# Four graph layers: layer 2's third step in T tiles, layer 3's results back to tokens by VectorE and DRAM

## The chip, the cores and the metric

The kernel runs on one core of one Trainium2 chip. The metric is the device time of one execution in microseconds, from a few runs; the median of three runs of the kernel before is 3717.38 us (3716.55 to 3718.34). A core has five engines that run their own instruction queues: TensorE (matmuls, PE in the profile), VectorE (DVE), ScalarE (ACT), GpSimd (POOL) and SyncE (SP), which here issues the DMAs.

## The reference

`x` is 64 graphs of 256 nodes with 256 features, `adj` their 0/1 adjacency. Four layers follow each other, each on h = relu(layernorm(x)), and each adds its result to x. Layer 0 is attention with 8 heads, layer 1 a graph attention with one head. What the change touches is layer 2 (a gated graph network of three steps) and layer 3 (graph attention with 4 heads of 64 features):

```python
def _gru_cell(inp, h, w_ih, w_hh, b_ih, b_hh):
    gi = inp @ w_ih.T + b_ih
    gh = h @ w_hh.T + b_hh
    i_r, i_z, i_n = jnp.split(gi, 3, axis=-1)
    h_r, h_z, h_n = jnp.split(gh, 3, axis=-1)
    r = sigmoid(i_r + h_r); z = sigmoid(i_z + h_z)
    n = tanh(i_n + r * h_n)
    return (1.0 - z) * n + z * h
# layer 2
for i in range(3):
    m = jnp.einsum('bnd,de->bne', h, weight[i])
    aggr = jnp.einsum('bst,bsd->btd', A, m)
    h = _gru_cell(aggr, h, w_ih, w_hh, b_ih, b_hh)
# layer 3
f = (einsum('bni,oi->bno', h, W) + b).reshape(B, N, H, c)
logits = leaky_relu(s_src[:, :, None, :] + s_dst[:, None, :, :], 0.2)
probs = softmax(where(adj[..., None] == 1, logits, -9e15), axis=2)
out = einsum('bijh,bjhc->bihc', probs, f).reshape(B, N, H * c)
```

## The kernel before

The 64 graphs go through in 32 pairs. A pair has 512 nodes, held as four groups of 128 (`T = 4`); half g of a pair is one graph. A "token" tile `[128, 4*256]` has nodes on the partitions and features along the row; a "T" tile `[128, 2*512]` has features on the partitions and the 512 nodes along the row. The matmuls are in float32 except the adjacency products of layer 2, which split h into three bfloat16 parts.

Nothing in the code gives the final order directly. Each layer function records tasks with `add` (engine, expected duration, buffers read and written), and `Plan.order` (L110) builds the order: at each point it takes, of the ready tasks, the one that by the planner's own model can begin first, with ties decided by a key. The key is the pair's number times `PERIOD` plus an offset per layer and kind of engine (`ON_PE`, `ON_SP`, `OTHERS`). `SLOW`, `MARGIN`, `BACK` and `SPARE` shape DMA latency, waits of SyncE, the choice between VectorE and GpSimd, and spare buffers; `RANKS` says where the preparation of the weights falls. A task with two forms (`evict`, `either`) can go to either of two engines, and the plan decides which. So several pairs are in work at the same time, and each engine has one fixed queue. SyncE issues all DMAs: inputs, outputs, rows broadcast to all partitions (`to_all`), and the turns.

A **turn** is a transposition of a whole `[128, 1024]` tile without TensorE. VectorE transposes blocks of 32x32 (`nc.vector.transpose`, L617 or L636), and `through_dram` (L603) writes the tile to a DRAM buffer (one DMA, L606) and reads it back so that the blocks change places (four DMAs, L609). Layer 0 uses eight a pair, layer 3 four, and layer 2 uses `turn_chunks` (L632) after its first two steps, so 14 a pair; the last pair uses TensorE in layers 2 and 3 (L1046, L627). A tile from `turn_chunks` has its columns in another order, marked `mixed`.

Layer 2, steps one and two, run in T form: `gate` (L964) makes a bank of gate sums for 128 features by 512 nodes, with the weights as the stationary operand, and the bias enters as a value per partition in ScalarE's activation (L981, L993, L1009, L1021). VectorE forms the rest (L998, L1005, L1026, L1031), and either GpSimd or VectorE the subtraction (L1014). The third step runs in token form (from L1052): the node tile is the stationary operand and the weights stream (L1066), 512 columns wide for r and z, 256 wide for the new gate. Biases then lie along the row and are added by VectorE from broadcast tiles `brz_bc` and `bhn_bc` (L1082, L1095, L1116). Half g needs only its own node groups, and its result goes straight into x (L1121, L1126, L1128, L1133).

Layer 3 (L1138) computes f for each group of nodes (L1159), makes the logits (Prelu, L1189), masks them and takes the row extreme (L659), exponentiates (L666), turns the result, and multiplies with f (L1211), which leaves features on the partitions. That product is evicted (L321), transposed to tokens by four TensorE transposes per half (`back`, L1227), multiplied by the reciprocal sums of the softmax (L1234), and added to x (L1239). The last pair runs a finer variant (`hT.fine`, `last`).

Of the kernel before, what the change touches and what calls it, by code (L numbers as in the profile page):

```python
# [16 lines left out]
P = 128  # L17
# [21 lines left out]
class Plan:  # L39
# [11 lines left out]

    SPARE, GRAIN = 4, 0.01
    SLOW, MARGIN = 1.3, 0.2
    BACK = {"DVE": 0.8, "POOL": 1.3}


    PERIOD, REST = 260.1, 0
    ON_PE = (128, 788, 5100, -4300)  # L60
    ON_SP = (3449, 2192, 2058, -4527)
    OTHERS = (100, -16, -1143, 1788)

    def __init__(self, slots, spare):
        self.slots, self.spare = slots, spare
# [121 lines left out]
def tile_adj_preln_d4(  # L187
# [43 lines left out]
        "f3": (2, [P, T, E3], FP, 0),  # L231
        "mask": (4, [P, T * N], BF, 1),
        "ps": (8, [P, 512], FP, 2),
        "w2": (4, [P, N2], FP, 2),
        "st": (4, [P, T, 6], FP, 1),
        "mv": (4, [P, T, 2], FP, 1),
        "rs": (4, [P, 2, T], FP, 1),
# [4 lines left out]
        "rows": (3, [T * H3, P], FP, 0),  # L242
        "dst": (4, [P, T, H3], FP, 0),
        "turn": (8, [P, T * N], FP, 0),
        "row1": (4, [N2], FP, 0),
        "row3": (4, [H3 * N2], FP, 0),
    }
# [13 lines left out]
    def held(name, shape):  # L261
        return const.tile(shape, FP, name=name)
# [6 lines left out]
    giT = held("giT", [P, NL, 2, 3 * D])  # L269
    whhT = held("whhT", [P, 2, 3 * D])  # L270
    brz, bhn, bih_sb, bhh_sb = held("brz", [P, 4]), held("bhn", [P, 2]), held("bih_sb", [P, 6]), held("bhh_sb", [P, 6])

    brz_bc = held("brz_bc", [P, N2])
    bhn_bc = held("bhn_bc", [P, 2, D])
    a1_sb = held("a1_sb", [P, 2, 2])
    blk = held("blk", [P, 2, 2, H3])
    nc.vector.memset(blk, 0.0)
# [4 lines left out]
    dram = ctx.enter_context(tc.tile_pool(name="dram", bufs=1, space=bass.MemoryType.DRAM))  # L282
    for tag, (n, shape, dtype, _) in SLOTS.items():
        if tag not in tiles:
            tiles[tag] = [(dram if tag in ("row1", "row3", "turn") else work).tile(shape, dtype, name=f"{tag}_{i}") for i in range(n)]
    plan = Plan({tag: v[0] for tag, v in SLOTS.items()}, {tag: v[3] for tag, v in SLOTS.items()})

    def buf(tag):
# [2 lines left out]
    def w4():  # L291
        return buf("w4")
# [7 lines left out]
    def dve(n):  # L300
        return 0.065 + n / 960.0
# [82 lines left out]
    def weights2():  # L384
# [45 lines left out]
        def halved():  # L430
# [5 lines left out]
        bhh_bc = w4()  # L436
        load_rows(brz_bc, b_ih[0:N2], (BN, 2))
        row = b_hh[0:N2]
        load(
            lambda: bhh_bc()[:, 0:N2],  # L440
            bass.AP(tensor=row.tensor, offset=row.offset, ap=[[0, P], [1, N2]]), bhh_bc,
        )
        add((V, dve(N2), lambda: nc.vector.tensor_add(brz_bc, brz_bc, bhh_bc()[:, 0:N2]), True), reads=[bhh_bc], writes=[(BN, 2)])
        load_rows(bhn_bc[:, 0], b_ih[N2 : 3 * D], (BN, 3))
        load_rows(bhn_bc[:, 1], b_hh[N2 : 3 * D], (BN, 4))

    def weights3():

# [183 lines left out]
    def turn_chunks(src, dst):  # L632

        e = w4()
        add(
            (V, dve(T * N) + 0.04, lambda: nc.vector.transpose(  # L636
                e().rearrange("p (b i x) -> p b x i", b=4, i=32), src().rearrange("p (x b j) -> p b x j", b=4, j=32))),
            reads=[src], writes=[e],
        )
        through_dram(e, dst)  # L640
        dst.mixed = True
# [268 lines left out]
    def layer2(xt, p):  # L910
# [47 lines left out]
                )  # L958
            return aT

        for l in range(NL - 1):
            r, hn, u = w4(), w4(), w4()

            def gate(us, terms, c0, o, claims=()):  # L964
# [88 lines left out]
        two = lambda ap, g: tok(ap())[:, 2 * g : 2 * g + 2, :]  # L1053

        def state(h, g):
            if h.mixed:
                return h().rearrange("p (m k t) -> p t k m", k=2, t=T)[:, 2 * g : 2 * g + 2]
            return two(h, g).rearrange("p t (k m) -> p t k m", k=2)

        bias = lambda i: bhn_bc[:, i : i + 1, :].to_broadcast([P, 2, D])  # L1060

        def tokens_mm(out, terms, t, c0, n):
            m = 0
            for w, src in terms:
                for k in range(2):
                    mm(out, chunk(src, k, t), w[:, k, c0 : c0 + n], start=m == 0, stop=m == 2 * len(terms) - 1)  # L1066
                    m += 1

        def new_gate(w, src, g, claims=()):
            ps = bank()  # L1070

            def product():
                for c in range(2):
                    tokens_mm(ps()[:, c * D : (c + 1) * D], ((w, src),), 2 * g + c, N2, D)

            add((PE, 1.74, product), reads=[src, HH, GI[l]], writes=[ps], claims=claims)
            return ps

        for g in range(2):
            ps = new_gate(whhT, hT, g, [hn])  # L1080
            add(
                (V, dve(N2), lambda g=g, ps=ps: nc.vector.tensor_tensor(two(hn, g), tok(ps()), bias(1), ALU.add)),  # L1082
                reads=[ps, BN], writes=[(hn, g)],
            )
        aT = messages(h)
        both = ((whhT, hT), (giT[:, l], aT))
        for g in range(2):
            for c in range(2):
                ps = bank()
                add(  # L1090
                    (PE, 3.44, lambda t=2 * g + c, ps=ps: tokens_mm(ps(), both, t, 0, N2)),
                    reads=[hT, aT, HH, GI[l]], writes=[ps], claims=[rz[g]],
                )
                add(
                    (V, dve(N2), lambda g=g, c=c, ps=ps: nc.vector.tensor_tensor(at_o(rz[g], c), ps(), brz_bc, ALU.add)),  # L1095
                    reads=[ps], writes=[(rz[g], c)],
                )
                add(
                    (A, act(N2), lambda g=g, c=c: nc.scalar.activation(at_o(rz[g], c), at_o(rz[g], c), AF.Tanh, scale=0.5)),
                    writes=[(rz[g], c)],  # L1100
                )
            gate_of = lambda g, i: tok(rz[g](), N2)[:, :, i * D : (i + 1) * D]

            add(
                (V, dve(N2), lambda g=g, gate_of=gate_of: nc.vector.scalar_tensor_tensor(
                    two(hn, g), gate_of(g, 0), 1.0, two(hn, g), ALU.add, ALU.mult), True),
                reads=[rz[g]], writes=[(hn, g)],
            )
            ps = new_gate(giT[:, l], aT, g)
            add(  # L1110
                (V, dve(N2), lambda g=g, ps=ps: nc.vector.scalar_tensor_tensor(
                    two(hn, g), two(hn, g), 0.5, tok(ps()), ALU.mult, ALU.add)),
                reads=[ps], writes=[(hn, g)],
            )
            add(
                (V, dve(N2), lambda g=g: nc.vector.tensor_tensor(two(hn, g), two(hn, g), bias(0), ALU.add), True),  # L1116
                writes=[(hn, g)],
            )
            add((A, act(N2), lambda g=g: nc.scalar.activation(two(hn, g), two(hn, g), AF.Tanh)), writes=[(hn, g)])
            add(  # L1120
                either(0.4 if h.mixed else 0.0, lambda eng, g=g: eng.tensor_sub(  # L1121
                    two(df, g).rearrange("p t (k m) -> p t k m", k=2), state(h, g),
                    two(hn, g).rearrange("p t (k m) -> p t k m", k=2))),
                reads=[h, (hn, g)], writes=[(df, g)],
            )
            add(either(0.0, lambda eng, g=g: eng.tensor_add(two(xt, g), two(xt, g), two(hn, g))), reads=[(hn, g)], writes=[(xt, g)])  # L1126
            add(
                (V, dve(N2), lambda g=g, gate_of=gate_of: nc.vector.scalar_tensor_tensor(  # L1128
                    two(df, g), gate_of(g, 1), 1.0, two(df, g), ALU.add, ALU.mult), True),
                reads=[rz[g]], writes=[(df, g)],  # L1130
            )
            add(
                (V, dve(N2), lambda g=g: nc.vector.scalar_tensor_tensor(  # L1133
                    two(xt, g), two(df, g), 0.5, two(xt, g), ALU.mult, ALU.add), True),
                reads=[(df, g)], writes=[(xt, g)],
            )

    def layer3(xt, p):  # L1138
        at, hT = norm_relu_T(xt, p)
# [36 lines left out]
        for g in range(2):  # L1176
# [121 lines left out]
```

## Time and profile before

| | |
|---|---|
| median of 3 runs | 3717.38 us |
| the profiled execution | 3717.08 us |
| its span, first to last instruction | 3715.3 us |
| mean granted TensorE clock | 0.993 |
| L971, gates of steps one and two (TensorE, 3072 records) | 722.1 + 715.1 us busy |
| L1066, all gates of the third step (2048 records) | 242.7 + 240.6 + 121.0 + 120.9 us busy |
| L617, blockwise transposes (VectorE, 380) | 466.3 us busy, mean 1233 ns |
| L636, the transposes of `turn_chunks` (VectorE, 62) | 126.1 us busy, mean 2034 ns |
| turns: DMA to DRAM / back | 442 of 512 KB / 1768 of 128 KB |
| mean share of the 16 DMA engines | 57.8% |

A group's row in the profile has its busy time, the mean duration of one record in ns, and the idle time of that engine just before its instructions, with the releaser that ended most of it. A float32 matmul in the code makes two records. Busy time counts a record from its start to a modelled end, and the next record may begin before that end; the time that a stretch of matmuls takes is read from the starts in the timeline.

### The profile page before, as it was taken

The page shows a single profiled execution, that of the slowest core. Times are in us where ns is not written, and L with a number is a line of the kernel's source. Part 1 is how long each engine was busy: PE and PEld are TensorE (multiplying, and loading weights), DVE is VectorE, ACT ScalarE, POOL GpSimd, SP SyncE. Part 2 cuts the span into 40 slices and gives each one's busy share as a digit, 9 for nine tenths or more (in the row PEclk, how much of TensorE's full clock was granted, in tenths as well). Part 3 has the DMA queues.
Part 4 walks back from the last instruction along what each step waited for, and adds up shares of the span by engine and source line. Part 5 has one row for each costly group of instructions (what it writes and reads, how often), then busy time and mean ns, then how long its engine had stood idle before and what let it go on. Part 6 is the DMA issues. An engine that isn't in the chain of part 4 may idle for free.

```text
span 3715.3 us, 56987 instructions
## 1 busy us (share of the span) xinstructions
PE 3657.9 (98%) x17377; PEld 2186.9 (59%) x17377; DVE 2881.1 (78%) x7648; ACT 2693.9 (73%) x7227; POOL 532.9 (14%) x494
## 2 busy tenths in 40 slices
PE   8999999999999999999999999999999999999997
PEld 5665565555656556565565656556565565655554
DVE  6877777887778877778877779877788777888765
ACT  6986666777677777777877768876777767777545
POOL 2001111111121101112011111111211111121000
PEclk8999999999999999999999999999999999999998
DMA  7783455756456664557646566565566645666322
GB/s 215 198 221 106 132 152 172 199 167 180 137 163 193 190 182 125 165 168 193 187 136 184 154 180 185 163 185 137 163 195 184 176 132 161 189 193 187 100 88 86
DMA packets 443970, 615.21 MB, mean 166 GB/s; under 512 B 44944, under 2 KB 374544, under 8 KB 443664
## 3 DMA queue, kind: packets, MB, share of 16 engines
q1 hardware_dynamic: 443664, 611.57, 57.8%
q8 instruction: 139, 2.28, 0.3%
q14 instruction: 167, 1.37, 0.1%
HBM read 362.56 MB, written 248.84 MB: 165 GB/s over the span
## 4 chain that ended last, share of the span: by engine, by line
PE 72%; ACT 13%; DVE 7%; DMA 5%; issue 1%; SPq 1%; POOL 0%; DVEq 0%; POOLq 0%; ACTq 0%
PE ps L971 24%; PE ps L1066 14%; ACT w L666 6%; PE ps L690 6%; PE ps L582 5%; PE ps L949 4%; PE ps L1159 3%; PE ps L553 3%; PE ps L883 3%; PE ps L710 2%; ACT w L741 2%; DMA w<-turn 2%; PE ps L760 2%; PE ps L1211 2%; PE ps L816 2%; DMA turn<-w 1%
## 5 line engine op out<-in xcount | busy, mean ns | idle before, releaser
L666 ACT ACTIVATE w<-w,mx 128x256 f32<-128x256 f32 x1536 | 758.7, 498 | 15.9 <-DVE mx L659 14.3
L971 PE MATMUL ps<-w,whhT 128*128 128x512 f32 x1536 | 722.1, 596 | 0.7 <-DVE w L1031 0.5
L971 PE MATMUL ps<-w,giT 128*128 128x512 f32 x1536 | 715.1, 594 | 0.0
L321 ACT COPY w<-ps 128x512 f32<-128x512 f32 (+1 forms) x564 | 318.9, 582 | 313.4 <-PE ps L690 99.8
L617 DVE STREAM_TRANSPOSE w<-w 128x1024 f32<-128x1024 f32 x380 | 466.3, 1233 | 66.3 <-ACT w L666 44.2
L659 DVE CUSTOM_DVE_ANT_0 w<-ps,mask 128x256 f32<-128x256 f32 x1024 | 369.5, 417 | 167.1 <-PE ps L710 166.5
L971 PEld LDWEIGHTS ps<-w,giT 128*128 128x128 f32 x1536 | 288.5, 190 | 337.8 <-issue 326.2
L971 PEld LDWEIGHTS ps<-w,whhT 128*128 128x128 f32 x1536 | 277.5, 190 | 279.2 <-issue 256.2
L741 ACT ACTIVATE w<-w,rz 128x256 f32<-128x256 f32 x896 | 381.5, 498 | 2.4 <-DVE rz L734 2.4
L1066 PE MATMUL ps<-whhT,w 128*128 128x512 f32 (+1 forms) x1024 | 363.6, 491 | 0.0
L1066 PE MATMUL ps<-giT,w 128*128 128x512 f32 (+1 forms) x1024 | 356.1, 486 | 0.0
L528 ACT ACTIVATE w<-x,rs 128x256 f32<-128x256 f32 x472 | 247.5, 591 | 96.4 <-DVE rs L520 92.6
L1014 POOL TENSOR_TENSOR w<-w,w 128x512 f32<-128x512 f32 x91 | 122.8, 1350 | 1187.9 <-ACT w L1009 1088.8
L666 ACT ACTIVATION_READ_ACCUMULATOR w<-w,mx 128x1 f32 x1536 | 292.3, 190 | 0.0
L1066 PEld LDWEIGHTS ps<-giT,w 128*128 128x128 f32 x1024 | 193.5, 190 | 149.0 <-issue 134.7
L659 DVE CUSTOM_DVE_ANT_0 w<-w,mask 128x256 f32<-128x256 f32 x512 | 200.5, 417 | 102.1 <-ACT w L1189 102.0
L949 PEld LDWEIGHTS <-w 128*128 128x128 bf16 x2304 | 243.5, 128 | 52.0 <-issue 32.8
L949 PE MATMUL ps<-mask,w 128*128 128x256 bf16 x2304 | 272.5, 274 | 0.0
L1066 PEld LDWEIGHTS ps<-whhT,w 128*128 128x128 f32 x1024 | 189.8, 191 | 116.0 <-issue 99.5
L514 POOL TENSOR_SCALAR rs<-mv 128x4 f32<-128x4 f32 x129 | 55.7, 432 | 1180.0 <-DVE mv L503 1131.9
L501 DVE BATCH_NORM_STATS2 st<-x 128x6 f32<-128x256 f32 x512 | 190.9, 415 | 41.4 <-DMA x<-in_x_dram 38.3
L1189 ACT ACTIVATE w<-w,f 128x256 f32<-128x256 f32 x512 | 222.8, 498 | 0.0
(130 smaller groups left out, 5783.5 us busy)
## 6 DMA issues: line engine op xcount, KB each, us to landing
turn<-w SPq DMA_DIRECT2D x442, 512.0 KB, 3.2
w<-turn SPq DMA_DIRECT2D x1768, 128.0 KB, 4.3
w<-in_adj_dram SPq DMA_DIRECT2D x128, 512.0 KB, 6.3
w<-row SPq DMA_DIRECT2D x64, 512.0 KB, 4.8
x<-in_x_dram SPq DMA_DIRECT2D x64, 256.0 KB, 5.6
out_dram<-x SPq DMA_DIRECT2D x64, 256.0 KB, 2.2
w<-row SPq DMA_DIRECT2D x32, 256.0 KB, 4.7
w<-in_L_gnn_weight_dram SPq DMA_DIRECT2D x3, 256.0 KB, 6.0
```

The source lines that it names most:

```text
L321: (A, act(n), lambda: nc.scalar.copy(dst(), src())),
L501: nc.vector.bn_stats(st()[:, t, :], tok(xt())[:, t, :])
L528: nc.scalar.activation(tok(xn())[:, t, :], tok(xt())[:, t, :], func, bias=rs()[:, 1, t : t + 1], scale=rs()[:, 0, t : t + 1])
L617: add((V, dve(T * N), lambda: nc.vector.transpose(blocks(), blocks())), writes=[e])
L659: nc.vector.tensor_tensor_reduce(row, src, mask, scale, 3.0e38, ALU.add, ALU.min, mn)
L666: nc.scalar.activation(row(e, r), row(e, r), AF.Exp, bias=mn()[:, r : r + 1], scale=-1.0, accum_out=zs()[:, z0(r) : z0(r) + 1])
L690: mm(ps(), w[:, k, o * P : (o + 1) * P], wide(hT, k), start=k == 0, stop=k == 1)
L741: op(row, row, rz()[:, r : r + 1])
L949: mm(ps()[:, g * N : (g + 1) * N], chunk_of(part(), h.mixed, t, o), tok(am(), N)[:, t, :], start=i == 0 and c == 0, stop=i == 2 and c == 1,)
L971: mm(ps(), w[:, k, c0 : c0 + P], wide(src, k), start=n == 0, stop=n == 2 * len(terms) - 1)
L1066: mm(out, chunk(src, k, t), w[:, k, c0 : c0 + n], start=m == 0, stop=m == 2 * len(terms) - 1)
L1189: nc.scalar.activation(dst, src, AF.Prelu, bias=f()[:, t, D + h : D + h + 1], alpha=ALPHA)
```

## The change

Layer 2's third step uses the T form of the first two: the loop runs over all `NL` steps. Its new h returns to tokens as after the other steps (`turn_chunks` for 31 pairs, TensorE transposes for the last), and is then added to x half by half by GpSimd or VectorE. The token form with its broadcast biases and their loads is removed.

In layer 3, for all pairs but the last, the product of a half is no longer transposed by TensorE. VectorE transposes its 32x32 blocks, one DMA writes the tile to a DRAM buffer `turn2`, four DMAs read it back so that nodes are on the partitions, and eight instructions per half (four heads for each of two groups of nodes) multiply by the reciprocal sum and add to x in one go.

The planner's constants are all different, and two more `w2` buffers replace the bias tiles.

```diff
-    SPARE, GRAIN = 4, 0.01
-    SLOW, MARGIN = 1.3, 0.2
-    BACK = {"DVE": 0.8, "POOL": 1.3}
-    PERIOD, REST = 260.1, 0
-    ON_PE = (128, 788, 5100, -4300)
-    ON_SP = (3449, 2192, 2058, -4527)
-    OTHERS = (100, -16, -1143, 1788)
+    SPARE, GRAIN = 5, 0.001
+    SLOW, MARGIN = 1.4, 0
+    BACK = {"DVE": 0.3, "POOL": 0.8}
+    PERIOD, REST = 954.6, 0
+    ON_PE = (-336, 2037, 8685, -4071)
+    ON_SP = (6411, 2547, 4387, -3182)
+    OTHERS = (2416, 34, -17, 3238)
...
-        "w2": (4, [P, N2], FP, 2),
+        "w2": (6, [P, N2], FP, 2),
+        "turn2": (4, [P, N2], FP, 0),
...
-    brz_bc = held("brz_bc", [P, N2])
-    bhn_bc = held("bhn_bc", [P, 2, D])
...
-        load_rows(brz_bc, b_ih[0:N2], (BN, 2))
...
-        load_rows(bhn_bc[:, 0], b_ih[N2 : 3 * D], (BN, 3))
-        load_rows(bhn_bc[:, 1], b_hh[N2 : 3 * D], (BN, 4))
...
-        for l in range(NL - 1):
+        for l in range(NL):
...
             if by_dma(l, p):
                 turn_chunks(u, h)
-                continue
-            for g in range(2):
+            for g in range(2) if not h.mixed else ():
...
-        l, rz, hn, df = NL - 1, [w4() for g in range(2)], w4(), w4()
...
+            if l == NL - 1:
+                for g in range(2):
+
+                    def to_x(eng, g=g, h=h):
+                        ap = h().rearrange("p (m k t) -> p t k m", k=2, t=T) if h.mixed else h().rearrange("p (t k m) -> p t k m", k=2, t=T)
+                        x4 = xt().rearrange("p (t k m) -> p t k m", k=2, t=T)[:, 2 * g : 2 * g + 2]
+                        eng.tensor_add(x4, x4, ap[:, 2 * g : 2 * g + 2])
+
+                    add(either(0.4 if h.mixed else 0.0, to_x), reads=[h if h.mixed else (h, g)], writes=[(xt, g)])
...
             add(evict(N2, oT, pso), reads=[pso], writes=[oT])
+            if not last:
+
+                e2, o, d = buf("w2"), buf("w2"), buf("turn2")
+                add(
+                    (V, dve(N2), lambda oT=oT, e2=e2: nc.vector.transpose(
+                        e2().rearrange("p (b x i) -> p b x i", b=4, i=32), oT().rearrange("p (x b j) -> p b x j", b=4, j=32))),
+                    reads=[oT], writes=[e2],
+                )
+                add((SP, 0.6, lambda d=d, e2=e2: nc.sync.dma_start(d(), e2())), reads=[e2], writes=[d], latency=3.2)
+                for b in range(4):
+                    add(
+                        (SP, 0.55, lambda b=b, d=d, o=o: nc.sync.dma_start(
+                            o()[32 * b : 32 * b + 32, :].rearrange("p (a w) -> p a w", a=4),
+                            d()[:, b * P : (b + 1) * P].rearrange("(a j) w -> j a w", a=4))),
+                        reads=[d], writes=[(o, b)], latency=3.0, claims=[rz],
+                    )
+                for c in range(2):
+
+                    def to_x(c=c, g=g, o=o, rz=rz):
+                        for h in range(H3):
+                            ap = o().rearrange("p (j a x i) -> p j x a i", j=2, a=2, i=32)[:, h % 2, 2 * (h // 2) + c]
+                            xh = tok(xt())[:, 2 * g + c, h * C3 : (h + 1) * C3].rearrange("p (a i) -> p a i", a=2)
+                            nc.vector.scalar_tensor_tensor(
+                                xh, ap, rz()[:, H3 * c + h : H3 * c + h + 1], xh, ALU.mult, ALU.add
+                            )
+
+                    add((V, H3 * 0.14, to_x, True), reads=[o, rz], writes=[(xt, g)])
+                continue
             psq, o = bank(), buf("w2")
...
-    RANKS = (1.7, 2.3, 1.2)
+    RANKS = (2.3, 1, 0.3)
```

More of the change, by code (lines that the diff above doesn't have):

```diff
@@ L284, in tile_adj_preln_d4 @@
         if tag not in tiles:
-            tiles[tag] = [(dram if tag in ("row1", "row3", "turn") else work).tile(shape, dtype, name=f"{tag}_{i}") for i in range(n)]
+            tiles[tag] = [(dram if tag in ("row1", "row3", "turn", "turn2") else work).tile(shape, dtype, name=f"{tag}_{i}") for i in range(n)]
     plan = Plan({tag: v[0] for tag, v in SLOTS.items()}, {tag: v[3] for tag, v in SLOTS.items()})
@@ L435, in weights2 @@
         add((V, 0.2, halved, True), writes=[BN])
-        bhh_bc = w4()
-        load_rows(brz_bc, b_ih[0:N2], (BN, 2))
[L438 to L443, printed above, removed]
-        load_rows(bhn_bc[:, 0], b_ih[N2 : 3 * D], (BN, 3))
-        load_rows(bhn_bc[:, 1], b_hh[N2 : 3 * D], (BN, 4))
     def weights3():
@@ L635, in turn_chunks @@
         add(
-            (V, dve(T * N) + 0.04, lambda: nc.vector.transpose(
+            (V, 1.8, lambda: nc.vector.transpose(
                 e().rearrange("p (b i x) -> p b x i", b=4, i=32), src().rearrange("p (x b j) -> p b x j", b=4, j=32))),
@@ L1049, in layer2 @@
                 add(evict(N2, lambda g=g, h=h: h()[:, g * N2 : (g + 1) * N2], ps), reads=[ps], writes=[(h, g)])
-        l, rz, hn, df = NL - 1, [w4() for g in range(2)], w4(), w4()
[L1053 to L1136, printed above, removed]
```

## The prediction

> **What bounds the kernel now.** I read the engine totals first, then the table of windows (busy time of each engine in stretches of the span), then the groups by line with shapes kept apart, and the timeline at two places.
>
> ```profile
> PE 3657.9 (98%) x17377; PEld 2186.9 (59%) x17377; DVE 2881.1 (78%) x7648; ACT 2693.9 (73%) x7227; POOL 532.9 (14%) x494
> ```
>
> ```profile
> 20.00:40.00 20.00, 17.30 (x113) 12.25 (x111) 12.80 (x68) 11.45 (x35) 1.26 (x2) 0.83 0.89 265
> 40.00:60.00 20.00, 13.26 (x52) 8.35 (x53) 14.54 (x50) 16.83 (x47) 10.02 (x10) 0.66 0.92 260
> ...
> 1600.00:2000.00 400.00, 398.33 (x1893) 239.70 (x1890) 311.19 (x817) 286.75 (x751) 64.80 (x59) 1.00 0.59 167
> ...
> 3640.00:3680.00 40.00, 34.49 (x150) 21.43 (x150) 31.61 (x77) 24.12 (x67) 3.15 (x5) 0.96 0.42 120
> 3680.00:3700.00 20.00, 14.07 (x44) 7.65 (x44) 8.21 (x34) 13.11 (x39) 0.00 (x0) 0.50 0.23 77
> ```
>
> After the times come PE, PEld, DVE, ACT, POOL, the granted clock, the DMA share and GB/s. In the middle TensorE stands still for 1.7 us in 400; of its 57 idle us (3715.3 - 3657.9) 17 lie in the first 60 us and some 21 in the last 75. So in the middle, time goes only where TensorE work goes; VectorE (78%) and ScalarE (73%) have room. But a busy PE row counts modelled ends, so I price TensorE work from start to start of rows that follow without a gap:
>
> ```profile
> L1066 PE MATMUL ps<-whhT,w 128*128 128x512 f32 x512 | 242.7, 596 | 0.0
> L1066 PE MATMUL ps<-giT,w 128*128 128x256 f32 x512 | 121.0, 379 | 0.0
> L1227 PE MATMUL ps<-ident,w 128*128 128x128 f32 x256 | 39.4, 276 | 2.2 <-ACT w L321 1.4 <-DVE w L322 0.8
> ```
>
> ```profile
> 3598.21 1.88 PE L1066 MATMUL ps<-giT,w 128*128 128x512 f32 x4
> 3599.93 0.60 PE L1227 MATMUL ps<-ident,w 128*128 128x128 f32 x4
> 3600.36 1.89 PE L1066 MATMUL ps<-giT,w 128*128 128x256 f32 x8
> 3602.09 1.88 PE L1066 MATMUL ps<-whhT,w 128*128 128x512 f32 x4
> ```
>
> Four matmuls of 512 columns take 1.72 us (0.43 each), eight of 256 take 1.73 (0.216 each), four transposes of 128 take 0.43, though their row says 0.60.
>
> **Layer 3's way back.** In 31 of 32 pairs the two groups of four L1227 transposes go (the last pair keeps its two). 62 x 0.43 = **26.7 us** of TensorE's own queue. By busy time it would be 62 x 39.4/64 = 38.2; I take 26.7, since the next matmul starts inside the row.
>
> [...]
>
> What comes instead, per half of a pair: one VectorE transpose of 128x512, one DMA to DRAM, four back, eight fused multiply-adds of 128x64. No row has the half-size transpose: half of the blockwise transpose L636 (2.034 us) is 1.02, half of the plain one L617 (1.23) is 0.6; L636 has the same pattern, so 62 x 1.02 = 63 us. For the fused instruction, the nearest small row is L520 (128x4, 0.176 us); 60 more elements at the rate of L998 (0.745 for 512) bring some 0.08, so 0.25 apart, less where the next one overlaps: 0.13 to 0.25, taken 0.2, so 496 x 0.2 = 99 us. [...] Either way VectorE pays more here than for what it loses: L1234 (43.2 us) and its part of L1239 (23.8). This costs nothing as long as VectorE stays below TensorE, so I add it up.
>
> **VectorE's sum.** Out with the old third step: L1082, L1095, L1105, L1111, L1116, L1121, L1126, L1128, L1133, together 424 us. In: half of what two steps now take in L998, L1005, L1026, L1031 (382, so 191), 31 turns of 2.03 (63), and the additions of h to x (31 x 1.07, as L1121 strided: 33; three more for L1014). Layer 3: -65, +162. The order of the two programs also shows the planner's re-assignment: 86 more normalizations on VectorE (L534, 0.37: +32), 244 more divisions (L741, 0.305: +74), some evictions (+5). Net +74, so 2955 of some 3690: 80%. ScalarE loses about as much by the same count (244 divisions and 86 normalizations out, 192 Tanh passes of the old step out, 254 biased ones in): -98, 70%. Neither bounds.
>
> **Layer 2's third step.** Before, a pair takes 32 records of 512 columns and 32 of 256: 32 x 0.43 + 32 x 0.216 = 20.7 us. After, 48 of 512: 20.6. Nothing, though there are a quarter fewer matmuls: TensorE pays by column. The weight loads lie under the matmuls in both. The results of 31 pairs return to tokens by the existing DRAM turn; the last pair uses eight more TensorE transposes (0.9 us, in the ending below).
>
> **DMA and SyncE.** Added: 31 whole turns of 0.52 MB each way and 62 half ones, 65 MB on 611.6. At the present rate the share of the DMA engines goes from 57.8 to 64%; the half turns read back in rows of 512 bytes instead of 1 KB, so up to 67%. SyncE's queue gets 465 more issues at 0.34 (L606) and 0.43 us (L609): 191 us, 6 us of a pair's 116. They stand in one queue, in order, with layer 0's and layer 3's turns, adjacency loads and outputs. A blocked head is nothing new there:
>
> ```profile
> SPq L790 <- ACT rows L321: 741.1, 62, 27.6
> SPq L606 <- DVE w L617: 452.4, 180, 41.2
> ```
>
> Yet TensorE waited 1.0 us in all for a turn. The new wait on VectorE is the fused group's, for the DMA back (issue, 3.2 us landing, four issues, 4.3 landing: some 10 us); what stands behind it is every later VectorE instruction, evictions for TensorE among them. Summed with the durations of these rows, VectorE's new order has 11 to 15 us of instructions between most transposes and their fused group, but some 4 to 6 in a tenth of them. So mostly covered; a late one costs up to 5 us on VectorE, at 20% spare. I take 0.
>
> **Smaller terms.** The order has 113 fewer changes from one matmul group to another, 62 of them the removed transposes. A change costs 0 to 0.1 us (a 512-column group after L1211 takes 1.82 instead of 1.72), so -3 (0 to -5). At the start 0.77 MB of broadcast biases go from a stretch where DMA is 0.9 busy: 3 us of transfer at 260 GB/s, mostly not waited for: -1 (0 to -3).
>
> At the end something is lost. Before, the token form finishes half g=0 of the last pair before its last gate matmul, and its layer 3 starts 2.8 us after that (3667.65 to L553 at 3670.45), the other half at 3679.47. In T form all gates must be done before either half returns: Tanh 0.68, two fused steps 1.4, transposes 0.9, eviction 0.6, addition 0.7, statistics 1.2, rstd 1.1, scaling 1.1 and hops. Half 0 is late by some 6 us, half 1 about as before. Pair 30's layer 3 softmax now stands here too (it fills the gap). ScalarE's softmax of half 0 then bounds the tail: **+5** (0 to +10).
>
> **Sum**, on the profiled execution's 3717.1 (span 3715.3 and 1.8 around it): -26.7 - 3 - 1 + 5 = 3691.4; the median of the runs is 0.3 higher, which changes nothing. **3691 us**. What I can't price is the order itself: all planner constants change. Its room for gain is the idle time between 60 and 3640 us, 19 us by the windows; its room for loss is open.
>
> **Rivals.**
> A, as summed: 3691, own range 3678 to 3703. Chance 0.60.
> B, the new order also takes idle time out of filling, middle and ending: all 19 us and no loss at the end gives 3667. For it: those waits hang on ScalarE and VectorE (L528, the mask of L806), whose loads are reshuffled. Against: 1.5 us per 400 is near the floor. 0.20.
> C, the transposes go, but half is given back in short waits because the chain of a pair is two DRAM trips (20 us) longer and buffers are held longer: 3691 + 13 = 3704. Against: pairs overlap. 0.12.
> D, slower: SyncE's queue becomes the limit. A turn that lands late (7.8 us at most against 4.2 in the median) or waits behind the new DMAs stalls TensorE 3.6 us. It decides from 26 us in all, or one stall in every fourth pair; one in every second is 16 x 3.6 = 58, so 3749. Against: SyncE spends most of its time waiting for producers, and fourteen trips a pair (442/32) have left 1.0 us of wait. 0.08.
> That the transposes don't go is excluded: the order holds 8 of 256.
>
> **Chances and range.** A measurement of this kernel tells 0.2% (7.4 us) from no change. Faster (below 3709.9): A and B whole, most of C: 0.87. Same: 0.06, C's and D's edges. Slower: 0.07. The range takes in B's end and C's: 3668 to 3711.
>
> **What would show it.** TensorE's busy time down by some 38 (busy rows) to about 3620, 99% or more in the middle windows, with the same 0.43 for a 512-column record; 8 transposes on the old back line; VectorE near 80% and fused rows of 0.13 to 0.25 us; DMA at 64 to 67%; longer idle time in the last 60 us. It is wrong if TensorE's waits for DMA or for VectorE in the middle windows exceed a few us per 400, or if the 512-column records of the third step don't run at 0.43.

## The result, and the profile after

| | before | after |
|---|---|---|
| median of 4 runs | 3717.86 us (3716.55 to 3719.21) | 3682.09 us (3680.70 to 3684.02) |
| the profiled execution / its span | 3717.08 / 3715.3 us | 3682.95 / 3681.2 us |
| mean granted TensorE clock | 0.993 | 0.993 |

The ratio is 0.9904 (95% interval 0.9887 to 0.9921): **35.8 us faster**, where 26.4 were forecast (3691 against 3717.4). So the direction and the range hold, and a quarter of the gain has no place in the sum. The engine totals of the kernel after, busy time first:

```profile
PE 3620.5 (98%) x16625; PEld 2056.2 (56%) x16625; DVE 2912.0 (79%) x8192; ACT 2573.7 (70%) x6950; POOL 529.0 (14%) x512
q1 hardware_dynamic: 510048, 675.82, 64.0%
```

TensorE's busy time is 37.4 us lower (38 forecast), VectorE's share 79%, ScalarE's 70%, and the queue of DMAs has 64.0% of 16 engines' span. All four were forecast to within a point. To find what was not forecast, the table of windows is the view to read. Its stretches are chosen here to separate the start, the filling, the middle and the ending. First the kernel before:

```profile
0.00:60.00 60.00, 42.61 (x192) 26.94 (x193) 33.78 (x145) 35.27 (x92) 19.64 (x26) 0.83 0.82 241
60.00:800.00 740.00, 733.54 (x3618) 441.70 (x3616) 576.92 (x1580) 556.45 (x1522) 92.89 (x88) 1.00 0.58 165
800.00:3400.00 2600.00, 2588.36 (x12344) 1546.58 (x12344) 2056.46 (x5450) 1933.82 (x5197) 397.39 (x356) 1.00 0.60 171
...
3534.00:3715.30 181.30, 160.08 (x631) 92.23 (x629) 108.00 (x249) 88.95 (x226) 10.32 (x12) 0.92 0.28 85
```

and the kernel after, in the same view:

```profile
0.00:60.00 60.00, 42.16 (x208) 27.43 (x209) 39.66 (x157) 40.38 (x112) 19.61 (x26) 0.89 0.82 237
60.00:800.00 740.00, 732.64 (x3497) 419.59 (x3496) 596.63 (x1698) 526.01 (x1446) 93.19 (x89) 1.00 0.63 180
800.00:3400.00 2600.00, 2600.00 (x11991) 1475.26 (x11990) 2110.78 (x5928) 1864.57 (x5049) 389.57 (x371) 1.00 0.67 192
...
3500.00:3681.20 181.20, 145.71 (x544) 79.08 (x542) 101.71 (x265) 87.80 (x220) 10.03 (x11) 0.91 0.36 106
```

TensorE's idle time is the stretch less the first busy figure. Over the whole span it hardly moves, 57.4 us before and 60.7 after, but it has changed its place. At the start it is 17.4 and 17.8, in the filling 6.5 and 7.4. In the middle it falls from 11.6 us to nothing at all: TensorE never waits in 2600 us. In the last 181 us it grows from 21.2 to 35.5. A total of idle time would have hidden both movements.

The second measure is the period, the time from one pair to the next in the middle. After, it can be read from the chain of waits, whose rows have the start, the duration and the number of joined steps. The same stretch of gates comes back 111.52 us later, which is 2157.84 - 2046.32:

```profile
2046.32 12.02 PE ps L959 x28
...
2157.84 12.02 PE ps L959 x28
```

Before, even and odd pairs follow at unequal distances, so I take a mean over 20 pairs (from the seventh to the twenty-seventh, by the starts of layer 1's product): 113.30 us. The same reading of the kernel after gives 111.52 again. A pair is 1.78 us cheaper, and the eight removed transposes should make only 0.86 of it (8 x 0.108). **The rest of this 1.78 is what the experiments look for.**

The rows of the new work, from the groups on VectorE with shapes kept apart:

```profile
L1154 DVE SCALAR_TENSOR_TENSOR x<-w,rz,x 128x64 f32<-128x64 f32 x496 | 105.4, 279 | 0.7 <-DMA w<-turn 0.7
L1136 DVE STREAM_TRANSPOSE w<-w 128x512 f32<-128x512 f32 x62 | 42.4, 685 | 26.2 <-ACT w L319 26.2
```

The fused instruction's records have a mean of 279 ns, but they overlap: 105.4 us over 496 are 0.21 us each. VectorE waited for the way back through DRAM 0.7 us in all, in a row that covers 31 pairs.

The ending shows what the larger idle time is. TensorE's timeline after the last gates (start, duration, and in brackets the idle time before, with its releaser):

```profile
3620.88 1.88 PE L959 MATMUL ps<-w,giT 128*128 128x512 f32 x4
3622.59 0.27 PE L1033 MATMUL ps<-ident,w 128*128 128x128 f32 x1
3625.05 0.98 PE L1033 MATMUL ps<-ident,w 128*128 128x128 f32 x7 [2.18 <-DVE w L1019]
3637.57 2.25 PE L541 MATMUL ps<-ident,w 128*128 128x128 f32 x8 [11.54 <-ACT w L516]
```

For 11.54 us TensorE waits for the last pair's normalization (L516), ahead of its layer 3. The timelines of ScalarE, GpSimd and VectorE, in this order, show why it is so late:

```profile
3626.59 3.70 ACT L1099 ACTIVATE w<-w,f 128x256 f32<-128x256 f32 x9
...
3634.13 2.89 ACT L1099 ACTIVATE w<-w,f 128x256 f32<-128x256 f32 x7
3636.92 1.08 ACT L516 ACTIVATE w<-x,rs 128x256 f32<-128x256 f32 x2
```

```profile
3628.53 0.75 POOL L503 TENSOR_TENSOR rs<-rs,mhalf 128x2 f32<-128x2 f32 x1
3632.10 0.23 POOL L502 TENSOR_SCALAR rs<-mv 128x2 f32<-128x2 f32 x1 [2.83 <-DVE mv L491]
```

```profile
3633.46 0.12 DVE L508 SCALAR_TENSOR_TENSOR rs<-mv,rs 128x2 f32<-128x2 f32 x1
```

GpSimd has the first half's reciprocal deviation ready at 3629.3 (3628.53 + 0.75). Meanwhile ScalarE works through pair 30's logits (L1099) and exponentials, and VectorE through its masks and a turn. These come first in their fixed queues. So VectorE takes the next step of pair 31 (L508) only at 3633.46, and ScalarE begins its scaling (L516) only at 3636.92. From the start of the last gate matmul to the start of the last matmul it was 41.6 us before and is 53.5 now. Before, the last gates, the first transposes of the last pair behind them, and the end were these:

```profile
3664.11 3.61 PE L1066 MATMUL ps<-giT,w 128*128 128x512 f32 x12
...
3670.45 0.33 PE L553 MATMUL ps<-ident,w 128*128 128x128 f32 x1 [0.85 <-ACT w L528]
...
3708.58 0.66 PE L1227 MATMUL ps<-ident,w 128*128 128x128 f32 x4 [0.69 <-ACT w L321]
```

### The profile page after: what moved, and what is told of

Read it like the earlier page. It is cut to its first block, busy times and chain, and to the rows that moved or that the text cites. A ratio compares the mean times of both kernels' runs of the same rounds, so it can differ in the third digit from the quotient of the medians.

```text
span 3681.2 us, 56370 instructions
## 1 busy us (share of the span) xinstructions
PE 3620.5 (98%) x16625; PEld 2056.2 (56%) x16625; DVE 2912.0 (79%) x8192; ACT 2573.7 (70%) x6950; POOL 529.0 (14%) x512
## 3 DMA queue, kind: packets, MB, share of 16 engines
q1 hardware_dynamic: 510048, 675.82, 64.0%
## 4 chain that ended last, share of the span: by engine, by line
PE 95%; ACT 2%; DVE 2%; DMA 1%; issue 0%; SPq 0%; DVEq 0%; ACTq 0%
PE ps L959 53%; PE ps L937 7%; PE ps L678 6%; PE ps L570 6%; PE ps L698 3%; PE ps L1069 3%; PE ps L1121 3%; PE ps L541 3%; PE ps L748 3%; PE ps L871 3%; PE ps L804 3%; ACT w L654 1%; PE ps L414 0%; DVE w L647 0%; ACT w L729 0%; PE ps L830 0%
## 5 line engine op out<-in xcount | busy, mean ns | idle before, releaser
L959 PE MATMUL ps<-w,whhT 128*128 128x512 f32 x2304 | 1083.7, 599 | 3.3 <-DVE w L1019 2.5
L959 PE MATMUL ps<-w,giT 128*128 128x512 f32 x2304 | 1068.4, 593 | 0.0
L959 PEld LDWEIGHTS ps<-w,giT 128*128 128x128 f32 x2304 | 433.0, 190 | 521.5 <-issue 487.9
L959 PEld LDWEIGHTS ps<-w,whhT 128*128 128x128 f32 x2304 | 418.8, 190 | 460.9 <-issue 438.1
L319 ACT COPY w<-ps 128x512 f32<-128x512 f32 x546 | 308.6, 580 | 181.5 <-PE ps L937 56.7
L997 ACT ACTIVATE w<-w,bih_sb 128x512 f32<-128x512 f32 x192 | 135.3, 717 | 287.0 <-DVE w L993 286.9
L729 ACT ACTIVATE w<-w,rz 128x256 f32<-128x256 f32 x652 | 284.8, 499 | 1.5 <-DVE rz L722 1.5
L981 ACT ACTIVATE w<-ps,brz 128x512 f32<-128x512 f32 x192 | 130.4, 679 | 202.9 <-PE ps L959 202.9
L986 DVE SCALAR_TENSOR_TENSOR w<-w,w 128x512 f32<-128x512 f32 x192 | 131.5, 685 | 146.1 <-ACT w L981 145.8
L516 ACT ACTIVATE w<-x,rs 128x256 f32<-128x256 f32 x386 | 206.3, 593 | 42.8 <-DVE rs L508 40.5
L1099 ACT ACTIVATE w<-w,f 128x256 f32<-128x256 f32 x512 | 227.9, 499 | 2.9 <-DMA w<-row 2.9
L553 ACT ACTIVATE w<-ps 128x512 f32<-128x512 f32 x184 | 102.7, 595 | 167.2 <-PE ps L541 167.0
L1009 ACT ACTIVATE w<-ps,brz 128x512 f32<-128x512 f32 x192 | 129.2, 673 | 128.3 <-PE ps L959 128.2
```

What stands on the lines that cost most here:

```text
L319: (A, act(n), lambda: nc.scalar.copy(dst(), src())),
L516: nc.scalar.activation(tok(xn())[:, t, :], tok(xt())[:, t, :], func, bias=rs()[:, 1, t : t + 1], scale=rs()[:, 0, t : t + 1])
L729: op(row, row, rz()[:, r : r + 1])
L959: mm(ps(), w[:, k, c0 : c0 + P], wide(src, k), start=n == 0, stop=n == 2 * len(terms) - 1)
L1099: nc.scalar.activation(dst, src, AF.Prelu, bias=f()[:, t, D + h : D + h + 1], alpha=ALPHA)
```

## Experiments

**The structure without its planner constants, and the constants without the structure.** First the whole new structure with the constants of before, and the old structure with the new ones.

```diff
-    SPARE, GRAIN = 5, 0.001
-    SLOW, MARGIN = 1.4, 0
+    SPARE, GRAIN = 4, 0.01
+    SLOW, MARGIN = 1.3, 0.2
...
-    ON_PE = (-336, 2037, 8685, -4071)
+    ON_PE = (128, 788, 5100, -4300)
...
```

> The whole change in structure, planned with the constants of the kernel before. Theory 1 (the gain is TensorE's removed transposes, whatever the order): 31 pairs x 0.9 us less, so about 3690 us, middle period of a pair near 112.4 us. Theory 2 (half of the steady gain is the new order, which took TensorE's gaps out): above 3695, gaps of 1 to 3 us per 400 us stay, as before.

> The structure of the kernel before, planned with the new constants. Theory 1: within some 8 us of 3718, since no TensorE work goes. Theory 2: the order alone takes gaps away, the period falls from 113.3 to some 112.4, and with a longer ending the time is 3700 to 3710.

Measured: the new structure with old constants 3758.21 us against 3715.53 in the same set, 1.0112 (1.0096 to 1.0129); the old structure with new constants 3729.60, 1.0034 (1.0021 to 1.0047). Each alone is slower than the kernel before, by 43 and 14 us. The first lies above 3695, as the theory of the order had it, but neither theory had it slower than before; the second fits neither theory. So the gain belongs to the pair of them, and the same TensorE instructions in another order cost 76 us more than the kernel after. In the first of the two, TensorE is busy for 2354.08 of the 2400 us from 800 to 3200. The table of TensorE's waits there (in total, times, longest) has no single culprit:

```profile
PE ps L959 <- ACT w L319: 10.1, 14, 2.8
PE ps L773 <- DVE dst L1081: 6.9, 3, 3.8
PE ps L830 <- DVE mask L794: 5.3, 6, 2.2
PE ps L959 <- DVE w L1019: 4.1, 3, 3.5
PE ps L541 <- ACT w L516: 4.1, 16, 0.9
PE ps L748 <- DMA w<-turn: 4.1, 3, 1.7
```

They are waits for VectorE and ScalarE at half a dozen places, and 4.1 us for a turn. TensorE has the same 16625 records as in the kernel after. The planner gave VectorE a little less and ScalarE more work (2871 and 2713 us busy, against 2912 and 2574), but neither is near the span. So what differs is mostly which instruction stands ahead of which; how much the other division of work adds isn't separated.

**Each half of the change with the constants of before.** In one kernel layer 3 is taken back to TensorE's transposes, in the other only layer 3 is changed:

```diff
-            if not last:
-                e2, o, d = buf("w2"), buf("w2"), buf("turn2")
...
-                continue
```

This is the first, against the kernel after; the second adds the same block, and the buffers `turn2`, to the kernel before.

> Only layer 2's third step in T tiles, layer 3 as before, constants of the kernel before. Theory 1: TensorE pays by column, so no steady gain; the ending is some 5 to 10 us longer: 3718 to 3728. Rival: the T form, with 160 us less VectorE work between TensorE groups, closes gaps: 3705 or less.

> Only layer 3's way back by VectorE and DRAM, third step in token form, constants of the kernel before. Theory 1: 3718 - 28 = 3690, with no change in the ending. Rival: the added VectorE work and turns put gaps into TensorE's middle and half of it is lost: 3704.

Measured: 3756.43 us (1.0108, 1.0093 to 1.0123) and 3776.85 us (1.0162, 1.0147 to 1.0178). Both are slower, by 41 and 61 us, which none of the expectations had, and together the halves cost 43, so they don't add up. With constants that belong to another structure, a part of a change can't be priced by leaving the rest out. The pricing must keep the order, or fit the order to each structure anew. The next runs do the one, then the other.

**The transposes, with the order kept.** To the kernel after, each half's product in layer 3 gets four transposes of the identity in front, whose result the product overwrites. The planner isn't told of them, so every engine's order stays.

```diff
             def product(...):
...
+                if not last:
+                    for i in range(4):
+                        nc.tensor.transpose(pso()[:, i * P : (i + 1) * P], ident, ident)
```

> The changed kernel in its own order, with four more TensorE transposes (of a constant, overwritten at once) ahead of each product of layer 3 in 31 pairs: 62 x 4. Theory 1 (TensorE's own time sets the pace): 62 x 0.43 = 27 us longer, 3709. Rival (the removed transposes were not worth their time, the gain is the order): less than 10 us longer, for the other engines give the slack back.

Measured: 3709.96 us against 3718.35 before, 0.9978 (0.9967 to 0.9989): 27.9 us above the kernel after's 3682.09 (26.5 by the profiled spans). The period rises from 111.52 to 112.39, by 0.87, which is 8 x 0.108. The group that was added, and the window from 800 to 3200 us:

```profile
L1119 PE MATMUL ps<-ident 128*128 128x128 f32 x248 | 37.7, 275 | 0.0
```

```profile
800.00:3200.00 2400.00, 2400.00 (x11163) 1372.82 (x11162) 1935.19 (x5428) 1707.98 (x4623) 355.96 (x339) 1.00 0.67 191
```

Its busy time is 37.7 us, and it costs 26.5 to 27.9: the reading from start to start was the right one. TensorE is busy all the time, so all other engines simply have a period that is 0.87 us longer. The transposes are worth some 27 of the 35.8 us, and the other half of the pair's 1.78 us has another cause.

**The same from the other side.** Of the kernel before's eight transposes per pair, two remain, and the order is kept. The kernel leaves three quarters of layer 3's results unturned.

```diff
-                for i in range(2):
-                    for k in range(2):
+                for i in range(2 if last else 1):
+                    for k in range(2 if last else 1):
```

> The kernel before in its own order, with one of the four transposes of layer 3's way back left in 31 pairs (three are left out, so three quarters of layer 3's result are not turned). Theory 1: 62 x 3 x 0.108 = 20 us shorter, about 3697. Rival (other engines bound that order too): less than 10 us shorter.

Measured: 3701.97 us, 0.9956 (0.9941 to 0.9970), so 16.4 us less instead of 20. The period falls by 0.33 to 112.97 instead of by 0.65. In the middle the removed work partly turns into waiting, as TensorE's waits from 800 to 3200 us show, first in the kernel before, then with fewer transposes:

```profile
PE ps L842 <- DVE mask L806: 8.4, 11, 1.0
PE ps L553 <- ACT w L528: 2.7, 11, 1.0
```

```profile
PE ps L842 <- DVE mask L806: 8.7, 11, 1.2
PE ps L553 <- ACT w L528: 6.3, 21, 1.5
```

The order of before has chains through VectorE and ScalarE that are as long as TensorE's own work in places. Where TensorE gets shorter, it meets them. In this order the removal of transposes doesn't pay in full.

**VectorE's and SyncE's new work.** Both runs keep the order of the kernel after. In one, every half-size transpose is done three times; in the other, SyncE issues four more DMAs of 64 KB per half, 248 in all, to DRAM that nobody reads.

```diff
-lambda oT=oT, e2=e2: nc.vector.transpose(...)
+lambda oT=oT, e2=e2: [nc.vector.transpose(...) for i in range(3)]
```

```diff
                     nc.sync.dma_start(d(), e2())
+                    for b in range(4):
+                        nc.sync.dma_start(spare_d[b], e2()[:, b * P : (b + 1) * P])
```

> The changed kernel in its own order, with layer 3's new VectorE transpose done three times over: 124 x 0.69 = 85 us more VectorE work, 79 to some 81% busy. If VectorE has room: within 4 us of 3682. If VectorE is next to bound: 10 to 40 us longer.

> The changed kernel in its own order, with four more DMAs of 64 KB to unused DRAM behind each of the 62 turns of layer 3: 248 more issues on SyncE at some 0.4 us (100 us in all) and 16 MB. If SyncE's queue and the DMA engines have room: within 4 us of 3682. If the queue is at its limit, as the slower rival said: over 10 us longer.

Measured: 3684.74 us (0.9909, 0.9893 to 0.9926) and 3682.23 us (0.9903, 0.9888 to 0.9918), against 3682.09 for the kernel after. Neither moves the time by more than the spread of its runs, and the period stays at 111.52. The tripled transposes raise VectorE's busy time from 2912 to 2993 us. So what was added to these engines in place of the transposes is covered, with room to spare.

**Each half with constants fitted to it.** The planner's constants, `RANKS` too, were chosen anew for each structure, for few waits of TensorE. Layer 3 alone, with the four `w2` buffers of the kernel before:

```diff
+    SPARE, GRAIN = 4, 0.05
+    SLOW, MARGIN = 1.30, 0.00
+    BACK = {"DVE": 0.30, "POOL": 0.50}
+    PERIOD, REST = 859.1, 0
+    ON_PE = (-336, 2037, 5067, -4300)
+    ON_SP = (6411, 2547, 7690, -3182)
+    OTHERS = (4396, -16, -1143, 2986)
...
+    RANKS = (2.2, 2.5, 1.2)
```

Layer 2 alone, with six:

```diff
+    SPARE, GRAIN = 5, 0.01
+    SLOW, MARGIN = 1.20, 0.10
+    BACK = {"DVE": 0.30, "POOL": 1.00}
+    PERIOD, REST = 859.1, 0
+    ON_PE = (-336, 2196, 8859, -4310)
+    ON_SP = (6411, -4928, 5848, -7138)
+    OTHERS = (10066, 34, -192, 3141)
...
+    RANKS = (2.5, 2.3, 0.0)
```

> Only layer 3's way back by VectorE and DRAM, third step in token form, four w2 buffers, with planner constants fitted to this structure. Theory (TensorE's removed time is the gain, and an order fitted to the structure is the condition for getting it): 3682 to 3695, near the whole change or better, for the token form gives the shorter ending. Rival (layer 3's way needs the T form beside it, for its relief of VectorE and its buffers): above 3705 however the constants are fitted.

> Only layer 2's third step in T tiles, TensorE's transposes in layer 3 kept, planner constants fitted to this structure. Theory: no TensorE work goes, so not below 3710; 3715 to 3735 with the longer ending. Rival (the T form closes TensorE's gaps, which was the half of the steady gain beyond the transposes): 3705 or less.

Measured: layer 3 alone 3703.95 us against 3719.29 (0.9958, 0.9943 to 0.9972), 15 us faster. Layer 2 alone 3701.28 us (0.9952, 0.9937 to 0.9966), 18 us faster. The two windows from 800 to 3200 us, layer 3 alone first:

```profile
800.00:3200.00 2400.00, 2385.47 (x11271) 1403.96 (x11271) 2006.13 (x5478) 1704.28 (x4640) 350.89 (x337) 1.00 0.62 181
```

```profile
800.00:3200.00 2400.00, 2399.28 (x11194) 1370.33 (x11194) 1919.48 (x5133) 1736.52 (x4683) 283.18 (x281) 1.00 0.64 182
```

These two rows decide most. Layer 2's T form alone, which takes no work from TensorE and keeps all its transposes, leaves it 0.7 us of waiting in 2400 where the kernel before has 11.6; its period is 112.16, 1.14 us under the kernel before. Layer 3's edit alone, though it removes some 27 us of transposes, has 14.5 us of waits there, and its period is 112.73, only 0.57 under. The first result is what the rival had forecast (3705 or less), against the theory that the T form is worth nothing. For the second, neither expectation fits, since the time lies between the two. In the T form, then, an order without gaps was found, and in the token form only one with about as many gaps as the kernel before has.

Two things remain open. The kernel before was never given newly fitted constants in its own structure, so the 18 us belong to the T form together with its fit, and how much a new fit alone would bring isn't shown. And layer 3 alone runs with four `w2` buffers, the whole change with six, though its new way back takes three per half: whether the buffers, the token form or constants not tried leave the gaps, these runs can't say.

**The new structure with other constants.** A second order for the whole change, with `BACK` for GpSimd at 0.70, the third value of `ON_PE` at 3958 and the first of `OTHERS` at 3504.

> The whole change with five of its planner constants moved a little (offsets of layer 2's TensorE work and of layer 0's other work, GpSimd's handicap). If the order is a fine fit, a small move costs or gains up to 10 us: 3672 to 3692. If only the structure counts: 3682 within 3.

Measured: 3684.62 us against 3719.29, 0.9906 (0.9889 to 0.9922). It can't be told from the kernel after. So the good order isn't a single lucky one.

**The ending.** The last pair alone gets the token form back in its third step; TensorE's order before that is untouched. Behind the added `return` stands the token form of the kernel before; its biases are loaded late, into spare `w4` tiles.

```diff
-        for l in range(NL):
+        for l in range(NL if by_dma(0, p) else NL - 1):
...
+        if by_dma(0, p):
+            return
+        biases, bhh_bc = w4(), w4()
...
```

> The changed kernel with its own constants, but the last pair alone takes its third step in token form as before (its biases are loaded late, into spare tiles); TensorE's order is the same up to that pair. Theory A (in T form both halves return late, which costs the 11 us by which the stretch from the last gate matmul to the end has grown): some 3671. Theory B (the growth is pair 30's layer 3 softmax standing ahead of the last pair's normalization in the queues of ScalarE and VectorE, whatever form the step has): 3678 to 3684.

Measured: 3678.69 us (3678.12 to 3679.12) against 3716.83 before, 0.9897 (0.9880 to 0.9913). It is the fastest version of the study, and the time is that of theory B: 3.4 us under the kernel after by the medians and 5.0 by the profiled spans (3676.2). From the last gate to the last matmul it is now 45.8 us, against 53.5 after and 41.6 before. TensorE's timeline there:

```profile
3620.99 1.89 PE L1078 MATMUL ps<-giT,w 128*128 128x256 f32 x8
3622.72 1.94 PE L1171 MATMUL ps<-w3a,w 128*128 128x264 f32 x8
3625.49 0.27 PE L773 MATMUL ps<-ident,dst 128*8 128x128 f32 x1 [0.83 <-DVE dst L1183]
3633.41 1.23 PE L541 MATMUL ps<-ident,w 128*128 128x128 f32 x4 [7.64 <-DVE w L522]
```

The first half begins its layer 3 (L1171) right behind the last gates, and so the 11.54 us are gone, as theory A would have it. But the second half now waits 7.64 us, for its normalization on VectorE. So both theories hold in part: the T form in the last pair costs a few us, and a part of the longer ending remains with the token form too. That this part comes from pair 30's softmax, which still stands ahead in the queues, is read from the timelines; no run took it away.

## Why the prediction was right, and where it was wrong

**The bound: right.** TensorE has no time left in the middle, and 0.87 us more work on it made each period 0.87 us longer. Tripling a VectorE step or adding 248 DMA issues changed nothing.

**Layer 3's way back, 26.7 us: right.** Put back alone in the same order, it costs 27.9 us by the medians and 26.5 by the profiled spans. A transpose costs 0.108 us here, and even so it belongs elsewhere, because the engine that does it is the only one without spare time: in the middle's 2600 us of the kernel after TensorE is busy for all 2600, VectorE for 2111 and ScalarE for 1865.

**VectorE's costs: right in the sum.** 2955 us were forecast and 2912 measured. The fused instruction at 0.21 us (0.2 taken) was right; the lower end of its range, 0.13, was an estimate that no row gives. The half-size transpose was taken as half of L636 because of its pattern, 1.02 us; it measured 0.685, so half of the plain L617 (0.6) was the nearer row. That is 21 of the 43 us too many, on an engine where they cost nothing.

**VectorE's wait, SyncE and DMA, 0: right.** Rival D is refuted, by the kernel after, where TensorE never waits in the middle, and by the run with more issues. SyncE's longest waits are still those for producers (the line L778 <- ACT rows has 736.9 us after, 741.1 us before in L790), and TensorE doesn't wait for it. The 67% that the shorter rows of the half turns might have cost didn't come: the queue of DMAs moved 285 GB/s of its busy share before (611.57 MB at 57.8%) and 287 after (675.82 MB at 64.0%). Rival C's short waits are absent from the kernel after; with the old constants, where TensorE stands still for 46 of 2400 us, they came, though mostly for VectorE and ScalarE and not for a turn.

**The order, which the sum left out: this is the step that failed.** The prediction put layer 2's third step at nothing and the order down as unpriceable, with idle time of 19 us as its room for gain, and gave rival B, which takes all of it, 0.20. As TensorE's work, layer 2's third step was rightly put at nothing. Added up from each matmul's start to the next one's, over the same 20 pairs as the period, the gates take 62.74 us a pair before and 62.83 after. But layer 2's T form with constants fitted to it was 18 us faster without any TensorE work removed. Rival B happened in part: the middle's 11.6 us went to zero, and the 0.7 before the ending too, while the start and the filling gained nothing.

What the room missed are gains that the trace doesn't show as idle. Per pair, of 1.78 us, 0.87 are the transposes, and 0.51 are visible waits (11.64 us in 2600, times 113.3). The remaining 0.4 can be placed by the same sums from start to start, though not explained. Most of it is layer 0's product of probabilities and values (L760, after L748), which falls from 4.05 us a pair to 3.73 with no idle time shown in either. Two such groups of the kernel before, and one of the kernel after, each with its neighbours:

```profile
830.44 1.94 PE L760 MATMUL ps<-w,w 128*32 128x256 f32 x32
832.30 1.99 PE L971 MATMUL ps<-w,whhT 128*128 128x512 f32 x4
...
846.05 0.33 PE L553 MATMUL ps<-ident,w 128*128 128x128 f32 x1 [0.16 <-ACT w L528]
846.30 2.46 PE L760 MATMUL ps<-w,w 128*32 128x256 f32 x32
848.69 0.66 PE L553 MATMUL ps<-ident,w 128*128 128x128 f32 x4
```

```profile
812.33 1.93 PE L748 MATMUL ps<-w,w 128*32 128x256 f32 x32
814.20 1.98 PE L959 MATMUL ps<-w,whhT 128*128 128x512 f32 x4
```

The first takes 1.86 us to the next start, the second 2.39, and the one after 1.87. Of the 40 groups before, ten are long like this (one of them, 3.90 us, while the granted clock was 0.57); after, none is. Their records overlap, so a delay between them isn't idle time. Beyond the visible waits, the adjacency products, the transposes of the normalization and other products of layers 0 and 1 take 0.5 us a pair less together, and the products for f in layers 1 and 3 and the gates 0.5 more. The term for fewer changes of groups (3 us) would be 0.1 a pair, and at its upper price of 0.1 us for each of the 113 changes it would be 0.35. But 62 added groups cost no more than their columns in the run with transposes added, which speaks against that price.

**The ending, +5: too small.** The path in the sum was right in kind (the first half late, ScalarE's softmax in the tail), but it had only the last pair's own steps in it. Half 0 was to be late by some 6 us; its transposes (L541) begin 15.4 us after the start of the last gate matmul, and began 3.1 us after it before, so it is late by 12. The idle time in the last 181 us grew by 14.3, and the way from the last gate to the last matmul by 11.9. By the timelines, that is this path with pair 30's softmax in front of it; the token form in the last pair gave back 5.0 us. The prediction saw that softmax there and counted it as filling for the gap, when it stands on ScalarE and VectorE ahead of what TensorE waits for.

**The start, -1:** nothing of it is seen in the idle time, which in the first 60 us is 17.8 after 17.4. The granted clock there was 0.89 after 0.83, and no run says what either made of the time.

**The sum as it came out**, from the profiled spans (-34.1): transposes -26.5, waits in the middle and before the ending -12.3, ending +14.3, start and filling +1.3; -10.9 remain, where -3 was forecast; that is about what the 0.4 us a pair that isn't idle time make over the pairs (some 12). Two errors of opposite sign, 12.3 gained and some 9 more lost at the end, nearly cancel. That is luck: that the time lies in rival A's own range (3678 to 3703) doesn't show that each of its terms was right. The miss that is left is mostly the part that wasn't idle time.

## What to carry to other kernels

Where every engine runs a fixed queue that a planner made, price a removed instruction in the same order (add it to the new kernel unplanned, and see whether the time grows by its columns), and price a change of structure only with an order fitted to it: here the same TensorE instructions took 3682 or 3758 us. Put an instruction on the engine that has room, even if it is dearer there: 0.87 us of TensorE a pair were worth a turn through DRAM. A form that costs the bound engine nothing more may still let the order close its gaps, and the last pair, which has nothing behind it to fill the gaps, may want another form than all others.

## What the runs showed of the hardware that I had not expected

Some VectorE instructions with two inputs in SBUF took longer when GpSimd worked beside them. In the timelines of VectorE and GpSimd in the kernel before:

```profile
1712.71 1.81 DVE L1026 SCALAR_TENSOR_TENSOR w<-w,w 128x512 f32<-128x512 f32 x1
...
1720.56 0.69 DVE L1026 SCALAR_TENSOR_TENSOR w<-w,w 128x512 f32<-128x512 f32 x1 [0.46 <-ACT w L1021]
```

```profile
1711.26 2.70 POOL L1014 TENSOR_TENSOR w<-w,w 128x512 f32<-128x512 f32 x2 [8.35 <-DMA turn<-w]
```

The same instruction takes 0.69 us alone and 1.81 us beside a GpSimd subtraction (two of them, 1711.26 to 1713.96): it ends at 1714.52, 0.56 us after GpSimd, which is most of its usual duration. Of the 128 records of L1026, the 39 that overlap a GpSimd tensor instruction have a mean of 1320 ns, and the others 678. Those of L1031, with two inputs as well, weren't longer beside GpSimd: the 15 that overlap have a mean of 690 ns, the other 113 of 689. Why the one line grows and the other doesn't isn't shown. What the views of one line give for this instruction (min/median/max in ns), before and after:

```profile
L1026 DVE SCALAR_TENSOR_TENSOR w<-w,w x128: 637/693/1819, 186.0 to 3640.3; 128x512 f32<-128x512 f32 x128
```

```profile
L1014 DVE SCALAR_TENSOR_TENSOR w<-w,w x192: 647/691/852, 199.0 to 3623.6; 128x512 f32<-128x512 f32 x192
```

After, its longest record is 852 ns. But another instruction has grown, the small L508 (L520 before, where three records were longer than 250 ns):

```profile
L508 DVE SCALAR_TENSOR_TENSOR rs<-mv,rs x129: 119/163/1482, 7.0 to 3637.9; 128x4 f32<-128x4 f32 x127, 128x2 f32<-128x2 f32 x2
```

25 of its records take some 1.48 us in place of 0.16, each while a GpSimd instruction runs. Added up over all VectorE records of over 1.25 times the median of their line and shape, the excess is 58 us before and 43 after, 33 of these in L508; it is 80 with the new structure in the old constants, and 30 with layer 2 alone fitted. So the good order keeps these two engines apart in the long instructions only. That TensorE's waits come from there isn't shown: with 43 us of excess on VectorE, TensorE doesn't wait in the middle at all.
